# Queueing a step's two VectorE additions together in the head attention of a gated attention block, with a larger margin for row maxima

## The chip, the cores and the metric

The kernel runs on one core of a Trainium2 chip. The metric is the device time of one execution in microseconds (us). It is one launch; the host only lays arrays out.

## The reference, cut to what matters

Eight batches of 1024 rows of width 512 go through two attentions, one after the other. The first is a cross attention with 8 heads of width 64 against a context of 1024 rows; the second is a self attention with 16 heads of width 32, whose output is weighted by gates. Both are exact softmax attentions in float32:

```python
sim = jnp.einsum('bihd,bjhd->bhij', q, k) * SCALE          # cross attention, 8 heads of 64
attn = jax.nn.softmax(sim, axis=-1)
out = jnp.einsum('bhij,bjhd->bihd', attn, v)
...
attn = jnp.einsum('bhqd,bhkd->bhqk', q_scaled, k) / math.sqrt(hd)   # head attention, 16 heads of 32
attn = jax.nn.softmax(attn, axis=-1)
h = jnp.einsum('bhqk,bhkd->bhqd', attn, v)
...
out = h * masked_gates.sum(axis=-1, keepdims=True)
```

Each softmax needs, for every query row, a maximum over the keys, the exponentials, their sum and a division.

## The kernel before, in words

**Chunks.** A batch is worked through in eight chunks: four of the cross attention (`kind == 1`, two heads each) and four of the head attention (`kind == 2`, four heads each, numbered 0 to 3 below). The maxima, the projections of q and k (L282) and other products of a *later* chunk are slipped in as fillers while a chunk's attention runs.

**Steps.** Keys lie on the partitions. A chunk of the head attention has two halves of the queries (h = 0 and 1, 512 queries each), and a half has eight steps s = 0 to 7, each with 128 keys. In a step:

- *scores* S(s), `score`, L500: TensorE first adds the row of negated maxima (`sh<-ones_b`), then q times k, into two PSUM tiles u = 0 and 1, two heads in each. There are two such tiles in all (`ps_sc`, bufs 2), so the scores of the next step wait for the exponentials of this one.
- *exponentials*, L511: ScalarE turns each of the two tiles into an SBUF tile `e` of 128 x 1024. There are nine `e` buffers.
- *values* V(s), `value`, L598: TensorE multiplies `e` with v.

The scores of step s+1 stand ahead of the values of step s. With V(s) of an even s, `paired` (L514) lets GpSimd add `e` of step s+1 onto `e` of step s, once for u = 0 and once for u = 1 (L516). I call these two the **pair of step s**, first and second. VectorE then adds the pair's two results onto two accumulators (`add`, L529); I call these the first and the second **addition**. Or, if `add` finds that VectorE has no time, the tile stays as an accumulator of its own and TensorE sums it at the end of the half (`summed`, L549).

**Maxima.** The maxima of the next chunk come from cheap bfloat16 scores (L413), two at a time into the three general PSUM tiles (`ps_gen`, bufs 3), which VectorE reduces (L454). After the last of them VectorE makes one tile of negated maxima (`nm`, L460), TensorE transposes it (`pr`, L465), ScalarE copies it out (`rows`, L467), and four DMAs on SyncE's queue write `sh` (L469). The next chunk's first scores need `sh`. I call this chain the **handover**. It runs from chunk to chunk.

**The order.** It is written out by hand at build time. A planner in the Python code keeps for TensorE, VectorE and GpSimd a sum of costs, `at`. Work that waits for another engine stands in a list `later` with a due time: `due(ns)` takes items from the head of that list while their due time is past; `room` forces them out when more than three accumulators would be live. `add` also puts an addition off by 300 planned ns, or turns it into an accumulator, by two tests: whether VectorE is planned to be free, and `ontime`, which comes from `in_time` in `attend` (L744): do the remaining maxima fit before the chunk ends, with a margin of 7000 planned ns? So a due time and a margin decide where an instruction stands in the engines' queues, and nothing is reordered when the program runs.

**Order in the program.** In batches 0 to 6 the head attention's order is the same in every batch; batch 7 has no next batch and so other fillers. I write chunk.half.step where needed: the pair of 1.1.4 is that of chunk 1, half 1, step 4.

Of the kernel before, what the change touches and what calls it, by code (L numbers as in the profile page):

```python
# [21 lines left out]
def tile_gated_block(  # L22
# [58 lines left out]
    work = ctx.enter_context(tc.tile_pool(name="work", bufs=2))  # L81
# [174 lines left out]
    at = {"PE": 0.0, "DVE": 0.0, "POOL": 0.0}  # L256
# [10 lines left out]
    def pe(ns):  # L267
        at["PE"] += ns
# [27 lines left out]
    class Chunk:  # L296
# [290 lines left out]
        def value(self, step):  # L587

            h, s = step
            width, st = self.width, self.st  # L590
            if s == 0:
                self.av = ps_av.tile([P, H], F32, tag="av", name=f"av_{self.key}_{h}")
            e = self.e[step]
            for kk in range(self.nk):
                kc = s * self.nk + kk
                for i in range(self.nh):
                    j = kk * self.nh + i
                    nc.tensor.matmul(  # L598
                        self.av[ts(i, width), :],
                        lhsT=st.v[:, kc, ts(self.c * self.nh + i, width)],  # L600
                        rhs=e[j // 2][:, j % 2, :],
                        start=(kc == 0),
                        stop=(kc == NT - 1),
                    )
                pe(1000)
                if kk == 0 and self.kind == 1:
                    room(1, self, h)
                    self.paired(h, s, 0, e[0], e[1], True)
                if kk + 1 < self.nk:
                    yield  # L610
            if self.kind == 2 and s + 2 == self.ns and self.ends:
                for u in range(2):
                    self.whole[h, u] = [e[u], self.e[h, s + 1][u]]
                live[0] += 4
                later.append((at["PE"] + 3000, self.summed, h, True))
            elif self.kind == 2 and s % 2 == 0:
                room(2, self, h)
                for u in range(2):
                    self.paired(h, s + 1, u, e[u], self.e[h, s + 1][u], u == 1)
            if s == self.ns - 1:  # L620
                nc.scalar.copy(st.hT[h][:, self.c, :], self.av)
                self.divided(h)
            if s % 2 or self.kind == 1:
                self.e.pop(step)
                self.e.pop((h, s - 1), None)
            yield "valued"
# [27 lines left out]
    later, soon = [], []  # L654
# [11 lines left out]
    def due(ns):  # L666
        while soon and soon[0][0] <= ns:
            _, emit, *args = soon.pop(0)
            emit(*args)
        while later and later[0][0] <= ns:  # L670
            if ns > 1e11:
                now()
            else:
                _, emit, *args = later.pop(0)
                emit(*args)

    def room(n, ch, h):

        while live[0] > 5 - n:
            if later:  # L680
                now()
            else:
                ch.summed(h, False)
        live[0] += n
# [13 lines left out]
    def run(g, ns):  # L698

        end = at["PE"] + ns  # L700
        while g and at["PE"] < end:
            if next(g[0], "end") == "end":
                g.pop(0)

    def pair(ch, slack):

        if ch is None or ch.mx is None or at["PE"] < ch.free:
            return False
        if ch.done + 2 < ch.pairs:
            if at["DVE"] - at["PE"] > (min(slack, 700) if part[0] else slack):  # L710
                return False
        ch.done += 1
        if next(ch.mx, "end") == "end":
            ch.mx = None
        return True

    def attend(
        ch, after, first, fillers, cost, maxima=None, ahead=None, since=0.0, rate=1.1, least=300
    ):

        filled, attended = 0.0, 0.0
        columns[0] = ch.width
        total = len(ch.steps) * (ch.SC + 1000 * ch.nk)

        def fill():
            nonlocal filled
            was = at["PE"]  # L730
            while fillers:
                if next(fillers[0], "end") == "end":
                    fillers.pop(0)
                elif ch.kind == 2 or not part[0]:
                    break
            filled += max(at["PE"] - was, least if at["PE"] - was < MM else 0)

        def pairs(slack):
            due(at["PE"])
            if maxima and maxima.mx:  # L740
                return pair(maxima, slack)
            return bool(ahead and ahead.done + 3 < ahead.pairs and pair(ahead, slack))

        def in_time(share):  # L744

            if not maxima or not (maxima.mx or maxima.waiting):
                return True
            pairs = maxima.pairs - maxima.done
            work = pairs * 1450 + 1750 + max(0, at["DVE"] - at["PE"])
            steps = (1 - share) * len(ch.steps) * (2 if ch.kind == 2 else 3)  # L750
            return pairs < 2 or pairs <= steps - 3 and work <= (1 - share) * (1.1 * total + cost) - 7000

        was = at["PE"]
        for got in ch.attention(after, first):
            attended += at["PE"] - was
            share = max(0, attended / total - since) / (1 - since)
            ontime[0] = in_time(attended / total)
            due(at["PE"])
            if got == "begun":
                fill()  # L760
            while got == "valued" and fillers and filled < cost * min(1, rate * share):
                pairs(0)
                fill()
            pairs(1100)
            while got == "ready" and (maxima.mx or maxima.waiting or fillers):
                if not pairs(1100):
                    if fillers:
                        fill()
                    else:
                        at["PE"] += 100  # L770
            was = at["PE"]
        if fillers and since:
            due(1e12)
        run(fillers, 1e9)
        columns[0] = HD2
# [326 lines left out]
    for b in range(B):  # L1102
# [5 lines left out]
        fill, cost = [], 0  # L1108
        if prev:
            one[2].loads()  # L1110
            fill, cost = [finish(prev, one[2].project(st))], 58 * MM
# [67 lines left out]
```

## Time and profile before

| what | value |
|---|---|
| median of three runs | 4916.66 us (4911.18 to 4921.75) |
| the profiled execution | 4917.12 us, its span 4915.3 us, mean granted TensorE clock 0.989 |
| TensorE busy | 4754.1 us, 97% of the span |
| VectorE busy | 3112.0 us, 63% |
| GpSimd busy | 2567.6 us, 52% |
| ScalarE busy | 2254.5 us, 46% |
| pairs on GpSimd (L516) | 764 of 2449 ns on the mean |
| VectorE additions (L529) | 427 of 1914 ns on the mean, shortest 1205, longest 3414 |
| reductions of two-at-a-time maxima (L454) | 2332 of 684 ns |
| sums on TensorE (L549), head attention's form | 1124 rows, 142.7 us busy |

How to read the profile: the busy share of an engine is a mean over stages. One batch takes some 608 us; in batch 2 the head attention runs from 1596 to 1862 us. A number in brackets behind a row of a timeline is the time for which the engine stood idle before it, with what it waited for. A TensorE matmul of float32 stands in two rows, and a row's duration overlaps with that of its neighbours, so costs below go from start to start.

### The profile page before, as it was taken

How to read it: one execution, taken by the hardware profiler on the slowest of the kernel's cores; microseconds unless marked ns; L12 is line 12 of the kernel's file. 1: busy time of each engine (PE TensorE's matmuls, PEld its weight loads, DVE VectorE, ACT ScalarE, POOL GpSimd, SP SyncE). 2: the span in 40 equal slices, each digit the busy share in tenths (PEclk: the TensorE clock that was granted, in tenths of full speed). 3: DMA queues.
4: the chain of work that ended last, by engine and by line, in shares of the span. 5: the costliest groups of instructions: out<-in, count | busy, mean ns of one | idle time of the engine just before them, and what ended most of it. 6: DMA issues, size and time to landing. Idle time of an engine off the chain costs nothing.

```text
span 4915.3 us, 83941 instructions
## 1 busy us (share of the span) xinstructions
PE 4754.1 (97%) x35196; PEld 1422.8 (29%) x35196; DVE 3112.0 (63%) x4225; ACT 2254.5 (46%) x2916; POOL 2567.6 (52%) x1346
## 2 busy tenths in 40 slices
PE   9999999999999999999999999999999999999998
PEld 2222232222322223222232222322223222232232
DVE  4557665576656865557655576555765567655664
ACT  3435634355343553435534355343552436524364
POOL 1635646366363663636636366363663636636474
PEclk9999999999999999999999999999999999999999
DMA  2020010200103001030010300102002020010100
GB/s 80 27 94 23 26 50 27 95 24 24 50 27 103 16 24 50 29 102 14 24 59 24 99 14 24 65 22 95 14 24 66 26 90 14 17 52 28 34 1 18
DMA packets 212683, 208.12 MB, mean 42 GB/s; under 512 B 24144, under 2 KB 147024, under 8 KB 212304
## 3 DMA queue, kind: packets, MB, share of 16 engines
q1 hardware_dynamic: 212016, 202.76, 13.0%
q8 instruction: 275, 4.51, 0.4%
q14 instruction: 104, 0.85, 0.1%
q10 hardware_dynamic: 288, 0.00, 0.0%
HBM read 153.93 MB, written 48.23 MB: 41 GB/s over the span
## 4 chain that ended last, share of the span: by engine, by line
PE 77%; DVE 12%; issue 3%; POOL 3%; ACT 2%; DMA 2%; SPq 1%; DVEq 0%; ACTq 0%; POOLq 0%
PE sc L500 20%; PE av L598 17%; PE po L282 9%; PE pq L282 8%; PE pm L413 7%; PE pk L282 6%; PE pv L282 5%; DVE mx L454 4%; DVE mx L437 4%; PE sum L549 4%; DVE e L529 3%; POOL e L516 2%; ACT e L511 1%; PE pn L282 1%; SPq L469 1%
## 5 line engine op out<-in xcount | busy, mean ns | idle before, releaser
L516 POOL TENSOR_TENSOR e<-e,e 128x1024 f32<-128x1024 f32 x764 | 1859.3, 2449 | 1122.9 <-PE av L598 660.4
L511 ACT ACTIVATE e<-sc 128x1024 f32<-128x1024 f32 x1536 | 1492.6, 1021 | 1222.7 <-PE sc L500 1186.0
L454 DVE TENSOR_REDUCE mx<-pm 128x1 f32<-128x512 f32 x2332 | 1484.8, 684 | 752.7 <-PE pm L413 709.0
L500 PE MATMUL sc<-q,k 32*128 32x512 f32 (+1 forms) x6144 | 1191.4, 604 | 0.0
L598 PE MATMUL av<-e,v 128*32 128x512 f32 (+1 forms) x6144 | 1086.2, 616 | 0.0
L529 DVE TENSOR_TENSOR e<-e,e 128x1024 f32<-128x1024 f32 x427 | 812.7, 1914 | 347.6 <-POOL e L516 346.7
L413 PE MATMUL pm<-kb,qb 32*128 32x512 bf16 (+1 forms) x3072 | 629.3, 383 | 64.9 <-DVE mx L454 34.4
L437 DVE TENSOR_REDUCE mx<-pm 128x2 f32<-128x1024 f32 x370 | 427.9, 1218 | 280.2 <-PE pm L413 280.2
L500 PEld LDWEIGHTS sc<-q,k 32*128 32x128 f32 (+1 forms) x6144 | 477.2, 189 | 205.5 <-issue 192.4
L500 PE MATMUL sc<-sh,ones_b 1*128 1x512 bf16 x3072 | 411.6, 385 | 32.3 <-ACT e L511 16.5
L413 PEld LDWEIGHTS <-qb 32*128 32x128 bf16 (+1 forms) x3072 | 152.7, 92 | 939.7 <-issue 929.3
L598 PEld LDWEIGHTS av<-e,v 128*32 128x32 f32 (+1 forms) x6144 | 194.0, 117 | 613.7 <-issue 594.5
L282 PE MATMUL pq<-y2T,wq 128*32 128x512 f32 x2048 | 259.5, 625 | 24.6 <-DVE y2T L242 21.8
L282 PE MATMUL pq<-y1T,wq 128*32 128x512 f32 (+1 forms) x1568 | 249.7, 600 | 6.5 <-ACT r L573 2.6
L282 PE MATMUL pv<-wv,y2T 128*32 128x512 f32 x2048 | 243.8, 602 | 2.6 <-DMA wv<-in_L_ffn_Wv 2.6
L282 PE MATMUL pk<-y2T,wk 128*32 128x512 f32 x2048 | 243.2, 595 | 0.0
L282 PE MATMUL po<-wp,h2T 128*64 128x512 f32 (+1 forms) x1152 | 231.1, 595 | 0.0
L282 PE MATMUL po<-wo,h1T 128*32 128x512 f32 x2048 | 223.0, 593 | 0.0
L500 PEld LDWEIGHTS <-ones_b 1*128 1x128 bf16 x3072 | 103.0, 91 | 386.4 <-issue 363.1
L549 PE MATMUL sum<-e,ones 128*32 128x512 f32 (+1 forms) x1380 | 209.7, 595 | 0.2 <-POOL e L516 0.2
L282 PE MATMUL pk<-ctx,wk 128*32 128x512 f32 (+1 forms) x1176 | 189.7, 606 | 19.6 <-DMA ctx<-in_ctx 6.0
L856 POOL TENSOR_TENSOR v<-v,bv_b 128x512 f32<-128x512 f32 x64 | 81.8, 1278 | 239.0 <-ACT v L855 239.0
(110 smaller groups left out, 2784.0 us busy)
## 6 DMA issues: line engine op xcount, KB each, us to landing
y<-xn SPq DMA_DIRECT2D x120, 256.0 KB
xb<-y SPq DMA_DIRECT2D x480, 64.0 KB
x<-in_x SPq DMA_DIRECT2D x64, 256.0 KB
out<-x SPq DMA_DIRECT2D x64, 256.0 KB
xs<-in_x SPq DMA_DIRECT2D x56, 256.0 KB
xn<-in_x SPq DMA_DIRECT2D x56, 256.0 KB
ctx<-in_ctx SPq DMA_DIRECT2D x7, 1536.0 KB
wq<-in_L_xattn_Wq SPq DMA_DIRECT2D x32, 256.0 KB
```

The source lines that it names most:

```text
L282: nc.tensor.matmul(ps[ts(j, w), :], lhsT=lhsT[:, ts(j, w)], rhs=rhs, start=start, stop=stop)
L413: nc.tensor.matmul(ps, lhsT=self.qb[ts(i, width), ts(c, P)], rhs=self.kb[ts(i, width), ts(kh, H)], start=True, stop=True,)
L437: nc.vector.tensor_reduce(out, tiles[u], AX.X, ALU.max)
L454: nc.vector.tensor_reduce(mx[:, i * NT + c, kh : kh + 1], ps, AX.X, ALU.max)
L469: nc.sync.dma_start(out=self.sh[r : r + 1, :].rearrange("o (c q) -> o c q", c=NT), in_=rows[ts(r // width, NT), :],)
L500: nc.tensor.matmul(pss[u][:, j % 2, :], lhsT=lhsT, rhs=rhs, start=(m == 0), stop=(m == 1))
L511: nc.scalar.activation(e[u], pss[u], AF.Exp)
L516: nc.gpsimd.tensor_tensor(one, one, two, ALU.add)
L529: nc.vector.tensor_tensor(accs[-1], accs[-1], a, ALU.add)
L549: nc.tensor.matmul(ps[ts(2 * u + j, self.width), :], lhsT=ones[:, 0 : self.width], rhs=acc[n][:, j, :], start=(n == 0), stop=(n == len(acc ...
L598: nc.tensor.matmul(self.av[ts(i, width), :], lhsT=st.v[:, kc, ts(self.c * self.nh + i, width)], rhs=e[j // 2][:, j % 2, :], start=(kc == 0 ...
L856: nc.gpsimd.tensor_tensor(st.v2[:, t, :], st.v2[:, t, :], bv_b, ALU.add)
```

## The change

In `value`, after the two calls of `paired` for the pair of an even step, the two newest items of `later`, which are the step's two additions, both get the due time at which the plan has GpSimd through with the second half of the pair (before, the first addition was due one pair half, 2350 planned ns, earlier). In `in_time`, the margin rises from 7000 to 9500 planned ns.

```diff
@@ value @@
                 for u in range(2):
                     self.paired(h, s + 1, u, e[u], self.e[h, s + 1][u], u == 1)
+
+                later[-2:] = [(at["POOL"], *item[1:]) for item in later[-2:]]
@@ attend, in_time @@
-            return pairs < 2 or pairs <= steps - 3 and work <= (1 - share) * (1.1 * total + cost) - 7000
+            return pairs < 2 or pairs <= steps - 3 and work <= (1 - share) * (1.1 * total + cost) - 9500
```

No arithmetic is changed. The two lines decide where in the four queues instructions stand.

## Prediction

> **What bounds the kernel now.** I read the page first, for the busy shares and the additions' group:
>
> ```profile
> PE 4754.1 (97%) x35196; PEld 1422.8 (29%) x35196; DVE 3112.0 (63%) x4225; ACT 2254.5 (46%) x2916; POOL 2567.6 (52%) x1346
> ...
> L529 DVE TENSOR_TENSOR e<-e,e 128x1024 f32<-128x1024 f32 x427 | 812.7, 1914 | 347.6 <-POOL e L516 346.7
> ```
>
> TensorE is the bound, so VectorE's time counts only where TensorE waits for it. Next I read TensorE's own waits:
>
> ```profile
> PE pm L413 <- DVE mx L454: 34.4, 76, 2.0
> ...
> PE sc L500 <- ACT e L511: 16.5, 17, 2.9
> PE sc L500 <- DMA sh<-rows: 11.6, 22, 1.8
> ```
>
> These are small sums, but the granted clock adds to them: its mean of 0.989 means some 54 us lost at half speed (0.011 x 4915). The timeline says where it goes. VectorE, then TensorE, at the border of chunks 0 and 1 in batch 2:
>
> ```profile
> 1660.17 3.22 DVE L529 TENSOR_TENSOR e<-e,e 128x1024 f32<-128x1024 f32 x1
> ...
> 1665.72 1.21 DVE L529 TENSOR_TENSOR e<-e,e 128x1024 f32<-128x1024 f32 x1
> ...
> 1668.05 3.35 DVE L529 TENSOR_TENSOR e<-e,e 128x1024 f32<-128x1024 f32 x1
> ```
>
> ```profile
> 1664.05 0.37 PE L413 MATMUL pm<-kb,qb 32*128 32x512 bf16 x1 [2.00 <-DVE mx L454]
> ...
> 1672.06 0.37 PE L413 MATMUL pm<-kb,qb 32*128 32x512 bf16 x1 [1.13 <-DVE mx L454]
> ```
>
> An addition takes 1.21 us alone and 3.2 to 3.4 where a pair runs on GpSimd (from 1659.97 and 1667.96): it waits for GpSimd's instruction. The reductions behind it come late, TensorE waits, and between 1660 and 1680 us its granted clock is 0.91. Of the head attention's additions, the 121 first ones take 2.56 us on the mean and the 114 second ones 1.87.
>
> **The change, part by part.** The two program orders, put side by side, show what moves. I price per batch, for the seven batches of one order.
>
> *a. Adjacent additions.* The first addition now follows the second half of its pair by the plan. From the pair's start at 0 (4.7 us long by its rows) and a full value, product, score and maxima step each, both additions stand 4.7 to 6.5 us later, nearly all clear of GpSimd. At the border above I counted the work from the score at 1653.16 to the one at 1678.61: its blocks take 20.2 us start to start, so 5.2 of 25.45 are lost, and 6.2 with the mean of the batches' clock dips (11 of 3.4 us in seven batches against this batch's one, at 1.7 lost each). Laid out with the same block times in the new order, the last two additions of chunk 0 still meet the next pair (it starts within a us of them), and a sum waits some 1.6 us for a PSUM tile. With a restart and half a dip 2.8 are lost: **gain 3.4**. Bounds: 1 (the stall only moves) and 6.2 (all of it).
>
> *b. Handover from chunk 1 to 2.* The larger margin stops additions earlier in chunk 1, so that its maxima end a step sooner; then the plan finds time again and adds 1.1.2 and the first half of 1.1.4. That last one frees the `e` buffer of the exponential 1.1.7 u = 1, and the first scores of chunk 2 wait for that exponential's PSUM tile. A new wait, then: behind this addition stand eight reductions on VectorE, behind the exponential ScalarE's whole queue. The old order has the same chain at the end of chunk 3:
>
> ```profile
> 1249.45 11.92 DVE L529 TENSOR_TENSOR e<-e,e 128x1024 f32<-128x1024 f32 x4 [2.89 <-POOL e L516]
> ```
>
> ```profile
> 1252.90 1.02 ACT L511 ACTIVATE e<-sc 128x1024 f32<-128x1024 f32 x1 [0.52 <-DVE e L529]
> ```
>
> ```profile
> 1253.98 0.39 PE L500 MATMUL sc<-sh,ones_b 1*128 1x512 bf16 x2 [1.15 <-ACT e L511]
> ```
>
> From V(4) at 1244.93 to that score are 9.05 us. In chunk 1 the pair starts later, for GpSimd first casts q and k (1.04 us each, at 1721.38 and 1722.37, and the pair then started 3.0 behind V(4), not 2.1; V(4) now comes 0.6 sooner): 10.5. With the rest of the score and a pair of maxima the next values start 11.4 behind V(4). Before it was 11.34 (1720.38 to 1731.72), with 2.9 of work that now lies elsewhere (sums 1.83, transpose 0.2, three pairs of maxima 0.9). **Loss 3.0**, and one clock window in place of 0.4, 1.0: 4.0. Bounds: 1.6 and 6.0. The wait for `sh` there (0.66 and 0.29 us) goes, since `pr` stands a step earlier, but what is late next is this exponential.
>
> *c. Handover from chunk 2 to 3.* Here `pr` moves the wrong way: it stood behind S(6), now behind S(7), with V(6) alone before the scores that need `sh`. The old order has this case in batch 7:
>
> ```profile
> 4815.60 0.28 PE L465 MATMUL pr<-ident,nm 128*32 128x128 f32 x1
> 4815.82 1.07 PE L598 MATMUL av<-e,v 128*32 128x512 f32 x8
> 4818.64 0.39 PE L500 MATMUL sc<-sh,ones_b 1*128 1x512 bf16 x1 [1.75 <-DMA sh<-rows]
> ...
> 4822.89 1.93 PE L598 MATMUL av<-e,v 128*32 128x512 f32 x8
> ...
> 4827.02 1.33 PE L598 MATMUL av<-e,v 128*32 128x512 f32 x8
> ```
>
> From `pr` to the values of the new chunk's first step are 11.42 us there, and 9.63 in batch 2 (1792.03 to 1801.66), which has V(5) and S(7) in it too (3.1 us by the rows from 1792.24 to 1795.35). **Loss 1.8 + 3.1 = 4.9.** SyncE's queue has the four copies in the same place, so nothing comes between. Of the 4.9, 2.0 are the half clock behind the wait (the rows from 4820.71 take 2.2, 1.9 and 2.3 us instead of 1.15, 1.0 and 2.1). Bounds: 2.9 and 5.3.
>
> *d. Maxima denser.* With the additions in a lump the plan puts more maxima on both sides of one score with a third PSUM tile held: 33 such places for 25. Each can cost 0.6 (0.23 us of wait in the waits on L454, the rest restart). I take a quarter, **1.2**; bounds 0 and 4.7.
>
> *e. Counts.* 434 additions for 427, 7 partial sums fewer, 28 rows fewer on TensorE at 0.127 us (142.7/1124): 3.6 us in all. The seven more additions (13 us) lie on VectorE, which is 63% busy; where the cover is gone, that is part of b. Some 0.7 a batch of waits for maxima early in chunk 3 (1205.66 in the waits) should go.
>
> *f. Batch 7.* Both its handovers come a step earlier: 1.75 + 0.29 + 0.15 and 0.62 + 0.30 us of waits for `sh` and part of their dips, of which I take 5 us.
>
> Sum: 7 x (-3.4 + 4.0 + 4.9 + 1.2 - 0.7) - 3.6 - 5 = 42.0 - 8.6 = **+33 us** on the profiled execution's 4917.1 (its span of 4915.3 and 1.8 around it), so 4950; the median of the runs shown lies 0.5 below that execution: 4950 rounded.
>
> On the clock, the trace has half-clock stretches right behind single waits of 1.1 to 2.3 us (1673.7 us behind the 1.13 above, 4820.8 behind the 1.75), and the terms above go by that. The Trainium skill speaks against it: its page "TensorE: Matmul & The Clock Gate", section "HAM oscillation — how this bites in real kernels", names only idle gaps above some 3.4 us. By the page, b and c would lose 3.0 and 2.9, a would gain some 1.8 less, and the sum would be an estimated 4942.
>
> **Rivals.** *Faster.* VectorE's relief is worth all that stands in a's upper bound, and the handovers cost no more than now, because the reductions, now seldom behind a blocked addition, end early enough for `pr` to find VectorE done. 7 x (-6.2 - 0.7) - 8.6 = -57: some 4860. For it speaks the 2.56 us of a first addition. Against it: `pr` has a fixed place in TensorE's queue, so early reductions don't move it. It decides at the handover to chunk 3: a wait under 1 us there and it is right. *No change.* The clock dips at a go altogether (6.2) while b takes its lower bound: 7 x (-6.2 + 1.6 + 4.9 + 0.6 - 0.7) - 8.6 = -7; some 4910. *Much slower.* b, c and d at their upper ends and a at 1: 7 x (-1 + 6.0 + 5.3 + 4.7 - 0.7) - 8.6 = +91; some 5010. *The change doesn't do what it says* in one respect already: more margin, and yet `pr` is later at chunk 3. That is in the forecast.
>
> **How the numbers follow.** Forecast (+12 to +60) 0.64, much slower 0.13, no change 0.11, faster 0.12. A measurement of this kernel tells 0.2%, some 10 us, from no change. Slower is the forecast and much slower, 0.77, with 0.11 for within 0.2% and 0.12 for faster. The range leaves out the faster rival and the end of the much slower one: 4907 to 4990.
>
> **What would show it.** Right: waits of scores for `sh` grow from 11.6 us, by some 1.5 in each of seven batches at chunk 3; waits of scores for ScalarE grow from 16.5 at chunk 2; the first additions' mean falls from 2.56 towards 1.5 us, and L529's 346.7 us behind GpSimd fall; the waits on L454 fall from 34.4; the mean clock falls a little. Wrong: chunk 3's scores start without a wait, or the exponential 1.1.7 isn't the last thing that chunk 2 waits for.

## The result, and the profile after

| | median | lowest to highest | profiled span | granted clock |
|---|---|---|---|---|
| before | 4915.90 us | 4911.18 to 4921.75 | 4915.3 us | 0.989 |
| after | 4999.07 us | 4997.88 to 5005.60 | 4996.7 us | 0.986 |

The changed kernel is slower: the ratio is 1.0175, interval 1.0162 to 1.0188. The forecast had the sign, 33 us of the 83, and a range that ended at 4990.

From the page after, the busy shares and the additions' group, then TensorE's own waits:

```profile
PE 4792.0 (96%) x35168; PEld 1433.7 (29%) x35168; DVE 3091.8 (62%) x4225; ACT 2245.8 (45%) x2909; POOL 2575.5 (52%) x1346
...
L529 DVE TENSOR_TENSOR e<-e,e 128x1024 f32<-128x1024 f32 x434 | 789.4, 1841 | 292.4 <-POOL e L516 291.3
```

```profile
PE sc L500 <- ACT e L511: 40.0, 26, 3.3
PE pm L413 <- DVE mx L454: 24.7, 92, 1.5
...
PE sc L500 <- DMA sh<-rows: 15.7, 17, 1.8
PE sum L549 <- DVE mx L454: 10.7, 7, 1.5
```

Every sign that the prediction named is there: VectorE waits less for GpSimd (291.3 for 346.7 us), TensorE waits less for maxima (24.7 for 34.4) and more for exponentials (40.0 for 16.5) and for `sh` (15.7 for 11.6). TensorE's four sums above grow by some 29 us together (the last of them was not there before), not 83: a wait in this view doesn't hold the half clock behind it, nor the work that it pushes elsewhere.

So I set the starts of the same exponentials side by side in the two traces, and took what each stretch of the head attention grew by. Mean of batches 0 to 6, us a batch, here for all kernels of this study:

| kernel | border 1.0.0 to 1.1.0 | handover to chunk 2 (1.1.0 to 2.1.4) | handover to chunk 3 (2.1.4 to 3.1.0) | 3.1.0 to the next batch |
|---|---|---|---|---|
| forecast (a; b and d; c; the rest) | -3.4 | 5.2 | 4.9 | -0.7 |
| **after** | **-3.4** | **10.1** | **8.0** | **-1.4** |
| queue line alone | -3.4 | 4.1 | 7.8 | -2.3 |
| margin 9500 alone | -0.2 | 0.9 | -0.1 | -0.7 |
| margin 12000 alone | -0.2 | 9.2 | 11.5 | -0.2 |
| after, ten `e` buffers | -3.3 | 8.7 | 7.1 | -2.6 |
| after, early `pr` at chunk 3 | -3.4 | 10.5 | 5.9 | -1.4 |
| after, both waits filled | -3.4 | 7.1 | 7.9 | -1.4 |
| after, no late additions | -3.4 | 2.4 | 0.1 | -1.6 |
| after, `nm` early | -3.4 | -0.1 | 0.0 | -0.8 |
| the same, late `pr` at chunk 3 | -3.4 | -0.1 | 5.3 | -0.8 |
| the same, late `pr`, filled | -3.4 | -0.1 | 3.1 | -0.8 |
| `nm` early, without the queue line | -0.4 | -2.0 | 0.2 | 0.0 |
| `nm` early, chunk 3's margin 13000 | -3.4 | 0.0 | 0.1 | -0.8 |

For after, 7 x (-3.42 + 10.08 + 8.02 - 1.42) = 92.8; batch 7 gives back 6.2 and the rest of the kernel 5.3: 81.3, the difference of the spans.

**The border, after.** VectorE in batch 2, then TensorE:

```profile
1684.85 2.35 DVE L529 TENSOR_TENSOR e<-e,e 128x1024 f32<-128x1024 f32 x2
...
1693.47 6.68 DVE L529 TENSOR_TENSOR e<-e,e 128x1024 f32<-128x1024 f32 x2
```

```profile
1700.80 1.06 PE L549 MATMUL sum<-e,ones 128*32 128x512 f32 x8 [1.52 <-DVE mx L454]
```

Two adjacent additions clear of GpSimd take 2.35 us together; before, one of them took 3.2. The last two meet the next pair and take 6.68, and a sum waits behind them.

**The handover to chunk 2, after.** GpSimd, VectorE, ScalarE and TensorE of the same stretch of batch 2, and the clock in two windows (the column behind POOL's busy time):

```profile
1749.12 2.04 POOL L398 CAST kb<-k 128x1024 bf16<-128x1024 f32 x1
1751.11 2.03 POOL L398 CAST qb<-q 128x1024 bf16<-128x1024 f32 x1
1753.11 10.24 POOL L516 TENSOR_TENSOR e<-e,e 128x1024 f32<-128x1024 f32 x4
```

```profile
1747.30 4.95 DVE L529 TENSOR_TENSOR e<-e,e 128x1024 f32<-128x1024 f32 x2
1755.49 3.34 DVE L529 TENSOR_TENSOR e<-e,e 128x1024 f32<-128x1024 f32 x1 [3.25 <-POOL e L516]
```

```profile
1758.93 1.94 ACT L511 ACTIVATE e<-sc 128x1024 f32<-128x1024 f32 x2 [4.28 <-DVE e L529]
```

```profile
1760.00 0.61 PE L500 MATMUL sc<-sh,ones_b 1*128 1x512 bf16 x2 [3.32 <-ACT e L511]
```

```profile
1748.00:1758.20 10.20, 8.56 (x59) 2.36 (x56) 6.95 (x3) 5.01 (x6) 10.20 (x6) 1.00 0.01 2
1758.20:1768.50 10.30, 8.50 (x44) 2.48 (x47) 4.50 (x7) 5.49 (x6) 5.14 (x2) 0.51 0.00 0
```

The chain is the one that the prediction laid out: casts, pair, the addition 1.1.4, the exponential 1.1.7, the score. TensorE stands for 3.32 us, and from 1758.2 us on its clock is at half for 10.3 us.

**The handover to chunk 3, after**, TensorE and its clock:

```profile
1834.32 0.39 PE L500 MATMUL sc<-sh,ones_b 1*128 1x512 bf16 x1 [1.80 <-DMA sh<-rows]
```

```profile
1836.00:1843.00 7.00, 6.87 (x33) 1.47 (x29) 0.00 (x0) 3.02 (x4) 1.30 (x1) 0.55 0.00 0
```

A wait of 1.8 us for `sh`, as in batch 7 of before, with 7 us near half clock behind it. A second thing has moved here. VectorE at the additions of the pair of 2.1.6, before and after, and GpSimd after:

```profile
1798.97 3.37 DVE L529 TENSOR_TENSOR e<-e,e 128x1024 f32<-128x1024 f32 x1 [9.16 <-POOL e L516]
```

```profile
1843.09 1.29 DVE L454 TENSOR_REDUCE mx<-pm 128x1 f32<-128x512 f32 x2 [13.22 <-PE pm L413]
1844.29 4.52 DVE L529 TENSOR_TENSOR e<-e,e 128x1024 f32<-128x1024 f32 x2
```

```profile
1844.42 6.60 POOL L516 TENSOR_TENSOR e<-e,e 128x1024 f32<-128x1024 f32 x2 [7.12 <-PE av L598]
```

Before, the first addition starts as soon as the first half of its pair is done. After, a pair of maxima, which stands behind S(1) of chunk 3, is ahead of it in the order. VectorE stands idle for 13.22 us until TensorE gets there, and both additions come just where GpSimd starts chunk 3's first pair. I call these two the late additions at chunk 3. In batches 1, 2, 4 and 6 the first of them starts 0.1 to 0.3 us ahead of that pair and takes 1.22 us. In batches 0, 3 and 5 the pair starts 0.1 us ahead of it; then both additions take 3.3 us or more, and TensorE waits 1.52 us for the reductions behind them. Chunk 3 loses 10.1 us in those three batches and 6.3 to 6.6 in the other four.

### The profile page after: what moved, and what is told of

It reads as the page before. It is cut to its first block, busy times and chain, and to the rows that moved or that the text cites. A ratio compares the mean times of both kernels' runs of the same rounds, so it can differ in the third digit from the quotient of the medians.

```text
span 4996.7 us, 83882 instructions
## 1 busy us (share of the span) xinstructions
PE 4792.0 (96%) x35168; PEld 1433.7 (29%) x35168; DVE 3091.8 (62%) x4225; ACT 2245.8 (45%) x2909; POOL 2575.5 (52%) x1346
## 4 chain that ended last, share of the span: by engine, by line
PE 78%; DVE 13%; ACT 3%; POOL 3%; issue 2%; DMA 1%; SPq 0%; DVEq 0%; ACTq 0%; POOLq 0%
PE sc L500 20%; PE av L598 17%; PE po L282 9%; PE pm L413 7%; PE pq L282 7%; PE pk L282 7%; PE pv L282 6%; DVE mx L437 4%; DVE mx L454 4%; DVE e L529 4%; PE sum L549 4%; POOL e L516 2%; ACT e L511 2%; DMA wv<-in_L_ffn_Wv 1%; PE pn L282 1%
## 5 line engine op out<-in xcount | busy, mean ns | idle before, releaser
L500 PE MATMUL sc<-q,k 32*128 32x512 f32 (+1 forms) x6144 | 1209.1, 610 | 0.0
L529 DVE TENSOR_TENSOR e<-e,e 128x1024 f32<-128x1024 f32 x434 | 789.4, 1841 | 292.4 <-POOL e L516 291.3
L413 PE MATMUL pm<-kb,qb 32*128 32x512 bf16 (+1 forms) x3072 | 637.6, 385 | 59.4 <-DVE mx L454 24.7
L282 PE MATMUL pq<-y1T,wq 128*32 128x512 f32 (+1 forms) x1568 | 249.7, 600 | 11.5 <-ACT r L573 5.4
L585 POOL TENSOR_TENSOR h2T<-h2T,r 128x512 f32<-128x512 f32 x62 | 79.1, 1276 | 296.7 <-ACT r L574 296.7
L549 PE MATMUL sum<-e,ones 128*32 128x512 f32 (+1 forms) x1352 | 211.5, 604 | 11.4 <-DVE mx L454 10.7
```

The lines of the kernel that those rows point to most:

```text
L282: nc.tensor.matmul(ps[ts(j, w), :], lhsT=lhsT[:, ts(j, w)], rhs=rhs, start=start, stop=stop)
L413: nc.tensor.matmul(ps, lhsT=self.qb[ts(i, width), ts(c, P)], rhs=self.kb[ts(i, width), ts(kh, H)], start=True, stop=True,)
L500: nc.tensor.matmul(pss[u][:, j % 2, :], lhsT=lhsT, rhs=rhs, start=(m == 0), stop=(m == 1))
L529: nc.vector.tensor_tensor(accs[-1], accs[-1], a, ALU.add)
L549: nc.tensor.matmul(ps[ts(2 * u + j, self.width), :], lhsT=ones[:, 0 : self.width], rhs=acc[n][:, j, :], start=(n == 0), stop=(n == len(acc ...
L585: engine.tensor_tensor(hT, hT, r, ALU.mult)
```

## The experiments

Theory P: the loss lies at the two handovers, each by the order there. Its rivals: the adjacent additions themselves cost (A), or the margin does (M). The kernel before, run again beside these kernels, had medians from 4914.04 to 4917.39 us; a difference of two kernels that ran at different times is no finer than that.

**One part alone.** The queue line with the old margin:

```diff
-... * (1.1 * total + cost) - 9500
+... * (1.1 * total + cost) - 7000
```

> Only the new line in value; the margin stays at 7000. The program order has the adjacent additions of chunk 0 and the late pr at chunk 3 of the changed kernel, but at chunk 2 pr stands behind S(7) with V(6) and two maxima ahead of the scores, and no addition stands ahead of the exponential 1.1.7. Theory P (the loss sits at the two handovers, each by its own order): border of chunks 0 and 1 -3.3 us a batch as in the changed kernel, chunk 3 +6.5 as there, chunk 2 some +4 (a wait for sh, less one pair of maxima of cover): 7 x 6 = some 4955 to 4970. Rival A (the adjacent additions cost by themselves, the margin nothing): 4999 as in the changed kernel. Rival M (the margin makes the whole loss and the line gains): below 4905.

Measured: 4955.05 us, ratio 1.0083 (1.0069 to 1.0097). The border and chunk 3 are those of the changed kernel, and chunk 2 loses 4.1 to a late `pr`. A and M fall. The late `pr` at chunk 3 comes from the queue line, for it is there with the old margin.

The margin without the queue line:

```diff
-                later[-2:] = [(at["POOL"], *item[1:]) for item in later[-2:]]
```

> Only the margin 9500; the additions keep their two due times. The program order differs from the kernel before in steps 0 to 2 of chunk 1, half 1 alone; both handovers are those of the kernel before. Theory P: no change, 4916 within 7 us. Rival M (the margin makes the loss): 4980 or more. Rival A: no change too.

Measured: 4915.46 us, ratio 1.0000 (0.9991 to 1.0009). The margin of 9500 by itself costs nothing; if a margin costs, it does so through the order that it brings about.

The same with a margin that does bring that order about, 12000:

> Only the margin, at 12000; the additions keep their two due times. The order has the late additions 1.1.2 and 1.1.4 with an early pr at chunk 2, and at chunk 3 pr behind S(7), as in the changed kernel, and no adjacent additions in chunk 0 and 1.0. Theory P (the order at the handovers costs, whoever brings it about; the border of chunks 0 and 1 stays as before): 4916 + 7 x (10 + 8 - 2) = some 5025, 5005 to 5040. Rival (adjacent additions are needed for the loss): 4930 or less.

Measured: 5059.47 us, ratio 1.0292 (1.0278 to 1.0306). Late additions and a late `pr` cost without any adjacent additions. The size was off (5005 to 5040 expected): chunk 3 lost 11.5 a batch, not 8, with more waits for maxima (55.0 us in all against 24.7). Here chunk 3's first pair is ahead of the late additions in all seven batches, which lose 11.4 to 11.7 each, where the changed kernel loses 10.1 in its three such batches. The 1.4 that remain were not taken apart.

**`nm` with the last maxima.** In `maxima`, the generator doesn't stop between the last reduction and `nm`, so that `pr` comes up one call earlier; the counts go down by one with it:

```diff
                 dve(2 * 690)
-                yield
+                if todo:
+                    yield
...
-        return self.nh // 2 * NT * NH + 2
+        return self.nh // 2 * NT * NH + 1
```

> Both lines of the change, and nm is emitted with the last reduction and not a turn of the planner later, so that pr stands a place earlier. In the program order the additions of chunk 1 no longer stand late (no addition ahead of 1.1.7), pr stands ahead of S(7) at chunks 2 and 3, the border of chunks 0 and 1 is that of the changed kernel. The handovers of the cross attention move too. Theory P: the border's -3.3 stays, chunk 2 and chunk 3 lose at most 1 to 2 each against before: 7 x (-3.3 + 2) - 6 = 4890 to 4915. Rival A: the handovers don't matter, 4985 to 5005. Theory W (the maxima now lie too densely ahead of the handover for ScalarE, whatever pr does): 4940 to 4970.

Measured: 4883.96 us, ratio 0.9939 (0.9926 to 0.9951): faster than both kernels. Its waits of scores for `sh` are almost gone, and its mean clock is 0.996:

```profile
PE sc L502 <- DMA sh<-rows: 0.8, 5, 0.2
```

The border's gain was in the changed kernel all along; the handovers ate it. What early `nm` is worth without the queue line shows in one more run:

> nm emitted with the last maxima and the margin 9500, but the additions keep their two due times. pr stands ahead of S(6) at both handovers, one place earlier than in the kernel before. Theory P (the adjacent additions are worth 3.3 to 4 a batch at the border of chunks 0 and 1, the handovers of the kernel before lose 1 to 2): some 4905, 4898 to 4912. Rival (the gain of the kernel with both lines and early nm comes from nm alone): 4884.

Measured: 4902.27 us, ratio 0.9970 (0.9958 to 0.9982). So early `nm` (with the margin of 9500) is worth some 14 us to the kernel before, and the queue line some 18 more.

**Chunk 2: the buffer.** A tenth `e` buffer; room is made elsewhere:

```diff
-    epool = ctx.enter_context(tc.tile_pool(name="epool", bufs=9))
+    epool = ctx.enter_context(tc.tile_pool(name="epool", bufs=10))
...
-                    part = work.tile([P, H], F32, tag="part", ...
+                    part = work.tile([P, H], F32, tag="r", ...
```

> Both lines of the change with the same order on the four engines, and a tenth e buffer; to make room, the tile of partial sums shares a buffer with the sums' reciprocal, and there is one buffer fewer for rows of the layer norms. The exponential 1.1.7 u = 1 then has a buffer without the addition 1.1.4. Theory P (the wait of the exponential for the addition makes chunk 2's loss, with the half clock behind it): the 3.3 us of wait and some 5 of clock go, chunk 2 loses 3 to 5 a batch and not 12: 4999 - 7 x 8 = some 4943. Rival B (the steps ahead of chunk 2 have no maxima and fillers left and run at ScalarE's pace): chunk 2 still loses 9 or more, 4980 to 5000.

Measured: 4973.35 us, ratio 1.0118 (1.0103 to 1.0134). The scores' waits for exponentials fall from 40.0 to 7.3 us in all, and yet chunk 2 still loses 8.7 of its 10.1; most of the 26 us lies elsewhere (1.1 a batch at the batch's end, 0.9 at chunk 3, where the late addition is now ahead of the pair in all seven batches). P in this form falls; B's range is missed too, by less. VectorE and then TensorE show why:

```profile
1747.79 3.37 DVE L529 TENSOR_TENSOR e<-e,e 128x1024 f32<-128x1024 f32 x1 [3.26 <-POOL e L516]
1751.08 2.47 DVE L454 TENSOR_REDUCE mx<-pm 128x1 f32<-128x512 f32 x4
```

```profile
1751.81 0.37 PE L413 MATMUL pm<-kb,qb 32*128 32x512 bf16 x1 [1.30 <-DVE mx L454]
```

The addition 1.1.4 itself waits 3.26 us for GpSimd and then takes 3.37 beside it; the reductions of chunk 3's maxima stand behind it in VectorE's queue, and TensorE runs out of PSUM tiles. A second wait had lain behind the first, on the same late addition. Against before, TensorE is idle 3.4 us more in this stretch and loses 2.7 more to half clock; 2.6 remain, and they may be B's steps at ScalarE's pace. No run separates these.

**The late additions.** So I took them away and left the denser maxima and the early `pr` of chunk 2 as they are:

```diff
-            return pairs < 2 or pairs <= steps - 3 and ...
+            return pairs < 1 or pairs <= steps - 3 and ...
```

> Both lines of the change, and in_time no longer answers yes when pr alone is left (it asks for fewer than one left, not two). The order up to the last maxima of chunk 1 is that of the changed kernel, its denser maxima and earlier sums too; the three late additions of chunk 1 are gone, its accumulators are summed on TensorE behind V(4), and pr of chunk 3 stands ahead of S(7). Theory P (the late additions at chunk 2 and the late pr at chunk 3 make the loss): 4999 - 7 x (8 + 7) = some 4895, 4885 to 4910. Theory W (the early end of the maxima and the steps without fillers behind it cost by themselves): 4930 or more.

Measured: 4892.03 us, ratio 0.9953 (0.9941 to 0.9966), 107 us under the changed kernel. Chunk 2 loses 2.4 in place of 10.1, so the late additions are worth 7.7 a batch there (with what eight sum matmuls and two pairs of maxima that come back give the bare steps to do); W falls. Chunk 3 loses nothing, as `pr` stands ahead of S(7), and no maxima stand ahead of the first addition of the pair of 2.1.6: in batch 2 it starts at 1793.35 us, beside the second half of its own pair, as before.

**Chunk 3: the place of `pr`.** In the kernel with early `nm`, `pr` of chunk 3 alone comes one call later (`turns` is 2 for it, 1 elsewhere):

```diff
-            yield
+            for _ in range(self.turns):
+                yield
             pr = ps_gen.tile([nh * NT, P], F32, tag="gen", ...
```

> The kernel with nm emitted with the last maxima (4884), and in batches 0 to 6 the transposition pr ahead of chunk 3 alone one turn of the planner later: behind S(7), with V(6) alone ahead of the scores, as in the changed kernel. Nothing else in the order of TensorE moves. Theory P (the place of pr makes chunk 3's loss, wait and half clock together): 7 x 7 more, 4925 to 4940. The size on record in the prediction (4.9 a batch): some 4918. Rival (chunk 3's loss in the changed kernel comes from the maxima and additions that moved around it): below 4895.

Measured: 4918.58 us, ratio 1.0007 (0.9999 to 1.0016), 34.6 us more than without: 4.9 a batch by the times (5.3 in the trace), the size on record and not P's 7. So some 3 of the changed kernel's 8.0 are not `pr`'s.

The same with eight matmuls in the wait that nobody reads:

```diff
+            if self.kind == 2 and self.c == 3 and step == (0, 0) and self.b + 1 < B:
+                warm = gen(f"warm_{key}")
+                for _ in range(8):
+                    nc.tensor.matmul(warm, lhsT=ones_b, rhs=self.kb[:, 0:H], start=True, stop=True)
```

> The same late pr, and ahead of the first scores of chunk 3 eight bfloat16 matmuls of 128x512 whose result nobody reads, some 1.7 us of TensorE that lie in the wait for sh. Theory C (of chunk 3's loss some 4 a batch is half clock that the idle TensorE brings on): that part goes, the wait stays: 4884 + 7 x 3 = some 4905. Rival (the half clock there has another cause, or the loss is the chain's length alone): as without the matmuls, 4925 to 4940, or more.

Measured: 4904.07 us, ratio 0.9981 (0.9973 to 0.9990), as expected. The span and mean clock, without and with the eight matmuls:

```profile
core 0: 4917.9 us, clock 0.990
```

```profile
core 0: 4899.9 us, clock 0.995
```

The chain to `sh` is as long as before, but TensorE isn't idle in it, and 2.1 of the 4.9 a batch go. In this stretch the time at half clock falls from 7.3 to 1.5 us a batch. So that part was half clock, and idle TensorE brought it on.

And the other way round, the changed kernel with `pr` of chunk 3 one place earlier and no other row of TensorE moved (`early` is true for chunk 3 in batches 0 to 6; its counts go down by one):

```diff
-                yield
+                if todo or not self.early:
+                    yield
...
-            self.free = at["DVE"] + 300
+            self.free = 0 if self.early else at["DVE"] + 300
```

> The changed kernel with pr ahead of chunk 3 one place earlier in batches 0 to 6, ahead of S(7) and not behind it; no other row of TensorE moves. Theory P by the run with the late pr alone (4.9 a batch): 4999 - 34 = some 4964, and what chunk 3 loses beyond that (8.0 a batch in the trace) stays, as it comes from the pairs of maxima and the additions that moved there. Rival (pr makes all of chunk 3's loss): 4999 - 7 x 8 = 4943. Rival (the late additions at chunk 2 make the whole loss): 4995 or more.

Measured: 4985.00 us, ratio 1.0139 (1.0125 to 1.0153): 14 us less, only 2.0 a batch, not P's 4.9; neither rival's time was met. VectorE, GpSimd and TensorE at the start of chunk 3:

```profile
1838.06 6.63 DVE L531 TENSOR_TENSOR e<-e,e 128x1024 f32<-128x1024 f32 x2
1844.61 2.64 DVE L455 TENSOR_REDUCE mx<-pm 128x1 f32<-128x512 f32 x4
```

```profile
1837.96 5.65 POOL L518 TENSOR_TENSOR e<-e,e 128x1024 f32<-128x1024 f32 x2 [2.23 <-PE av L600]
```

```profile
1845.34 1.18 PE L414 MATMUL pm<-kb,qb 64*128 64x512 bf16 x2 [1.52 <-DVE mx L455]
```

The wait for `sh` is nearly gone (1.2 us in all), and chunk 3's first pair now starts 0.1 us ahead of the late additions in all seven batches, not in three. They take 6.63 us beside it, and TensorE waits 1.52 for the reductions behind them, with a clock dip again. By themselves the late `pr` costs 5.3 a batch in the trace and the late additions, with the maxima ahead of them, 5.9. Together they cost 10.1 where the pair is first and some 6.4 where the addition is, 8.0 on the mean. What tips this 0.1 us one way or the other was not taken apart.

**Both waits filled**, in the changed kernel:

```diff
+            warm = self.kind == 2 and self.c in (2, 3) and step == (0, 0) and self.b + 1 < B
+            for n, half in enumerate([order] if self.kind == 1 else [order[:1], order[1:]]):
+                if warm and n == 3 - self.c:
+                    ps = gen(f"warm_{key}")
+                    for _ in range(14 if self.c == 2 else 8):
+                        nc.tensor.matmul(ps, lhsT=ones_b, rhs=self.kb[:, 0:H], start=True, stop=True)
```

> The changed kernel with matmuls that nobody reads in the two waits of batches 0 to 6: 14 bfloat16 matmuls of 128x512 (3.0 us) between the two halves of chunk 2's first scores, 8 (1.7 us) ahead of chunk 3's. Theory C (behind the waits lies half clock worth 2.9 a batch at chunk 2 and 4.1 at chunk 3, which idle TensorE brings on): between 4999 - 7 x 7 = 4950 and, if a third of it stays as in the earlier filled run, 4967. Rival (the half clock is not due to the idle time): 4995 or more.

Measured: 4979.81 us, ratio 1.0131 (1.0117 to 1.0145). This lies outside theory C's 4950 to 4967 and short of its rival's 4995. Chunk 2 gains 3.0 a batch, as expected of its clock. Chunk 3 gains 0.1: its half clock goes down by 2.0, and TensorE's idle time from chunk 3's first exponential on grows by 1.1. Here chunk 3's first pair is ahead of the late additions in six of the seven batches: the same exchange as in the run before.

**A better order.** Early `nm`, and chunk 3's margin at 13000, so that the six additions of its second half, which stand late too, come a step earlier:

```diff
-... * (1.1 * total + cost) - 9500
+... * (1.1 * total + cost) - (13000 if ch.c == 3 else 9500)
```

> The kernel with nm emitted with the last maxima (4884), and in chunk 3 alone a margin of 13000, which puts its six late additions a step earlier, further ahead of the exponentials that need their buffers at the end of the batch. Theory P (late additions delay an exponential there, 1.15 us of wait, and some half clock): 1.5 to 3 a batch gained, 4865 to 4875. Rival (the additions only move their wait): 4880 to 4890. Rival (late additions cost by their number, and there is one tile more on TensorE): 4890 or more.

Measured: 4883.72 us, ratio 0.9933 (0.9919 to 0.9946), the same as with early `nm` in the changed kernel: P falls, and the rival by which the additions only move their wait fits.

## Why the prediction was wrong in size

- **a, right.** -3.4 forecast, -3.42 measured, and the sum's new wait of 1.6 is 1.52. The half dip of the clock that the forecast had there did not come, so the agreement is in part luck. Besides, the first additions' mean fell from 2.56 to 2.20 us only, not towards 1.5: late ones beside a pair make up for early ones.
- **b and d, the step that failed most.** 5.2 forecast, 10.1 measured. The chain was right: from V(4) to the waiting score are 11.09 us (1748.91 to 1760.00), 10.5 forecast, as the casts took 2.04 and 2.03 us beside the additions of 1.1.2 and not 1.04. Three other sizes were off. I counted the work that left the steps from V(4) on, three pairs of maxima and the sums; from V(3) on it is five pairs and eight sum matmuls, some 3.8 us (sums 1.83, a pair 0.4), and they made the half before dense. I took one clock window, 1.0; there were two, and three in batch 2, 2.9 by the same count. And I gave the new addition no cost but the buffer's wait: with ten buffers, where TensorE waits for the reductions behind the same addition, chunk 2 still loses 8.7. Of the 10.1, 7.7 go with the late additions, and 2.4 stay with the denser half. In the trace, 5.2 of the 10.1 are more idle time of TensorE, 2.9 more half clock, and 1.9 remain, which no run separates.
- **c, right for what it counted, incomplete.** `pr` alone is 4.9, as forecast, of which filling its wait takes off 2.1 (2.0 of half clock forecast). What c left out, at no cost, is a pair of maxima that the new order puts ahead of the first addition of the pair of 2.1.6: it holds both additions back until chunk 3's first pair runs. With them chunk 3 loses 8.0. The queue line does this without the new margin, the margin of 12000 does it without the queue line, and with early `nm` the two lines of the change don't do it.
- **e, the sentence behind both.** "The seven more additions (13 us) lie on VectorE, which is 63% busy; where the cover is gone, that is part of b." What cost was not their 13 us but their place. The three new ones of chunk 1 stand beside GpSimd's casts and a pair, at 2.97, 2.05 and 3.34 us in batch 2, and those of chunk 3 are old ones that come late, beside a pair, with reductions behind them. That is the stall which a removes at the border, and I didn't look for it where the change moved additions to. The wait for maxima early in chunk 3 that should go did not: it is 0.70 to 0.73 us in all seven batches after. The 1.4 a batch gained from 3.1.0 on stand in its place in the sum, which is luck.
- **f, about right.** -5 forecast, -6.2 measured in the four stretches.
- **The rivals.** The much slower one (+91) came nearest in time, but not by its reasons: a kept its whole gain, and chunk 3 went past c's upper end of 5.3, because that bound didn't have the late additions in it.
- **The clock.** The Trainium skill, page "TensorE: Matmul & The Clock Gate", section "HAM oscillation — how this bites in real kernels", names only idle gaps above some 3.4 us. Here the half clock follows waits of 1.75 us, and filling such a wait in seven batches takes 14.5 us off the kernel; the measurement decides.

## What to carry to other kernels

When a change moves an operation that is slow beside another engine, look up what runs beside it at its new place and what is queued behind it there, not only at the place that it left. A wait that one removes may lie on top of another on the same instruction: take the instruction away as well as its wait before pricing it. Look at what was put ahead of it in its own queue as well: a wait can come from there though the operation itself has not moved. And where an order is made by due times and margins, price the order, row by row at every handover: the margin of 9500, which moved no handover by itself, cost nothing.

## What the runs showed of the hardware

- **The blocking goes both ways.** The casts of `kb` and `qb` take 1.04 us elsewhere (median of 64) and 2.04 and 2.03 beside VectorE's additions at chunk 2, while those two take 4.95 together, not 2.4. The Trainium skill, page "SBUF — State Buffer", section "SBUF: two separate sides", has this as an exclusive lock between GpSimd and a VectorE instruction with two inputs from SBUF, by which whoever comes second waits. The durations agree with it: these two casts and two additions take turns, and after the first addition each ends 0.9 to 1.1 us behind the end of the one before.
- **A tenth of a microsecond decides who is blocked.** At chunk 3 of the changed kernel an addition that starts 0.1 to 0.3 us ahead of GpSimd's pair takes 1.22 us, and one that starts 0.1 us behind it 3.34 us. Chunk 3 lost 6.3 to 6.6 us the first way and 10.1 the second. So a wait that one removes ahead of such a place can come back by turning the two round, as it did with the early `pr` and with the filled waits.
- **The same wait, different dips.** With the late `pr` alone, a wait of 1.74 to 1.76 us at the same place is followed by 3.4 us of half clock in one batch, 6.8 in four and 10.2 in two. A single dip is no measure of what such a wait costs; its mean over batches is.
